# A graph network's attention edges, placed 17 tiles later: 27 chunks instead of 26

## The chip, the cores and the metric

The kernel runs on one core of one Trainium2 chip. TensorE (PE in the profile; its weight loads are PEld), VectorE (DVE), ScalarE (ACT), GpSimd (POOL) and SyncE (SP) are five engines with a queue each; they meet through semaphores. The metric is the time of one execution on the device, in microseconds; a kernel's time is the median over several executions.

## The reference

A graph has 6250 nodes with 128 features and 100000 edges, sorted by their destination. Destinations are drawn as 6250·u², so that low nodes have many edges and high ones few. Two relational layers come first (not touched by the change except that the lists for attention are made beside the first of them), and then two layers of graph attention, each followed by a batch normalization over the nodes and an ELU:

```python
src = jnp.concatenate([edge_index[0], loops])      # 100000 edges and 6250 self loops
dst = jnp.concatenate([edge_index[1], loops])
...
e = leaky_relu(al_s[src] + al_d[dst], 0.2)         # 4 heads
m = segment_max(e, dst)
ee = jnp.exp(e - m[dst])
den = segment_sum(ee, dst)
alpha = ee / den[dst]
out = segment_sum(alpha[:, :, None] * xw[src], dst)
...
mu, var = x.mean(0), x.var(0)                      # batch normalization, over all nodes
h = elu(gamma * (x - mu) * rsqrt(var + EPS) + beta)
```

## The kernel before

**Lists.** `gat_list` merges the sorted edges with the self loops into one list of 106250 entries, ordered by destination, and cuts it into tiles of 128. The constant `NT` = 832 is the number of tiles, `TC` = 32 the tiles of a chunk, `NCH` = 26 the chunks. 831 tiles hold entries; the last one is padding. `windows` finds for each group of `GQ` = 4 tiles the first node that it adds to, and counts how many passes over the list are needed (`passes_g`): one as long as the nodes of a group fit a window of `WA` = 68 columns; one more is added when the last chunk begins at a node below `SETTLED` = 5760, because the statistics of the batch normalization are taken of those nodes before the last chunk is summed. `chains` makes masks per chunk. All three are generators, stepped once in each half-group of the first relational layer (`rgcn`, `next(others, None)`), between that layer's own instructions. `rgcn` also fetches a row of relations per half-group into the tile `relT` (L733, four buffers) from SP's queue, three half-groups ahead.

**An attention layer** (`gat`, once for each of the two layers) has a fully unrolled loop over the chunks. Three things are written for a chunk k:

- `gathers(k)`: one indirect DMA a tile on POOL's queue (`gather`, L615), each bringing 128 rows of 136 numbers from the table in HBM into the tile `v`. `v` lies in two halves of 16 tiles; the pool `grp` has six buffers, so that three chunks have room. A half's buffer comes free when the chunk three before has been read from it.
- `softmax(k)`: a long chain of small instructions, mostly on DVE, with a few on PE and ACT between them. It begins with ACT's copies L853 and PE's transposes L855 of the whole chunk, so that the chunk's last gather must have landed; DVE's first instruction of it is L860; it ends with DVE L947 and the transposition L949 of the weights `w`.
- `sums(k)`: DVE weights eight tiles at a time (`weight`, L958) and makes one-hot selections (`selections`, L627); PE multiplies each tile with its selection (L974) into a bank for four tiles; DVE adds each bank to the sums (`add`, L961). It needs `softmax(k)`.

The order on the engines is that of the code (`in_order`): in loop k the gathers of chunk k+1 are written first (POOL runs as far ahead as the buffers allow), then 16 steps of `sums(k)`, two tiles a step; from the eighth step on, a piece of `softmax(k+1)` follows each step. The weights' transposition L949 of chunk k+1 is so the end of loop k. Only the next-to-last loop is different: there all of `sums` is written first, then the batch normalization's statistics (`bn_stats`, L1065) of the first 5760 nodes, 18 instructions, and then the last softmax by itself. After the last chunk follow two more instructions of statistics, `bn_factors` and the ELU.

Before the loops, `gat` copies one column per chunk into `snaps` (L1022, with register loads in between), takes the selections of the first tiles, and runs `gathers(0)` and `softmax(0)` with nothing beside them.

Of the kernel before, what the change touches and what calls it, by code (L numbers as in the profile page):

```python
# [8 lines left out]
F32 = mybir.dt.float32  # L9
# [28 lines left out]
ES = ER * SC  # L38
NT = 832
TC = 32  # L40
NCH = NT // TC
NP = NT // SC
G = 16
# [16 lines left out]
NS = 320  # L60
SETTLED = 18 * NS
FAR = 1e6
EPS = 1e-5
# [17 lines left out]
class Gnn:  # L81
# [214 lines left out]
    def gat_list(self, scratch):  # L296
# [3 lines left out]
        n = self.stage().bitcast(I32)  # L300
        nc.vector.tensor_scalar(n, self.self_d, float(N), None, op0=ALU.min)
        d = self.stage().bitcast(I32)
        nc.vector.tensor_scalar_add(d, n, float(KOFF))
        nc.vector.scalar_tensor_tensor(d, d, KDST, n, op0=ALU.logical_shift_left, op1=ALU.bitwise_or)
# [28 lines left out]
        nc.vector.tensor_scalar(cols(dst_i), turned, KDST, None, op0=ALU.logical_shift_right)  # L333
        self.dst = scratch[:, 5 * SW:5 * SW + NT]
        nc.vector.tensor_scalar(self.dst, dst_i, -float(KOFF), float(N), op0=ALU.add, op1=ALU.min)
# [6 lines left out]
    def windows(self, scratch):  # L342
# [9 lines left out]
        for q in range(NQ):  # L352
            first = dst[0:1, q * GQ * NP:(q * GQ + 1) * NP]
            nc.vector.tensor_copy(self.base[:, :, q], first)
            ps = self.ps()[:, :NP]
            nc.tensor.matmul(ps, self.ones, first, start=True, stop=True)
            w = slice(q * GQ * NP, (q + 1) * GQ * NP)
            of_group = lambda v: v.rearrange("e (c p) -> e c p", p=NP)
            nc.vector.tensor_sub(of_group(self.ahead[:, w]), of_group(dst[:, w]), ps[:, None, :].to_broadcast([P, GQ, NP]))
            starts.append((w, first))  # L360
# [12 lines left out]
        nc.vector.tensor_reduce(count[:, 1:2], steps, AX.X, ALU.add)  # L373
        c = column(NT - TC)
        nc.vector.tensor_scalar(count[:, 0:1], dst[0:1, c:c + 1], float(SETTLED), None, op0=ALU.is_lt)
        nc.vector.tensor_add(count[:, 1:2], count[:, 1:2], count[:, 0:1])
        self.passes_g = const.tile([1, 1], I32, name="passes")
        nc.vector.tensor_copy(self.passes_g, count[:, 1:2])
        yield
        nc.vector.tensor_copy(by_tile(firsts), by_place(dst[0:1, :]))  # L380
        nc.vector.memset(lasts[:, 0:1], -1.0)
        for w, first in starts:
# [16 lines left out]
    def chains(self, scratch):  # L399
# [35 lines left out]
        nc.vector.memset(self.cut[:, :, P:], 0.0)  # L435
        for k in range(0, NCH, 2):
            z = slice(k, k + 2)
            yield
            nc.vector.tensor_scalar(ri[:, z], ri[:, z], KDST, None, op0=ALU.logical_shift_right)
            nc.vector.tensor_scalar_mul(rows[:, z], ri[:, z], BIG)  # L440
            nc.vector.tensor_sub(self.cut[:, z, 1:P], rows[:, z, :P - 1], rows[:, z, 1:])
            for mask, e in ((self.head, 0), (self.tail, P - 1)):
                nc.vector.tensor_tensor(mask[:, z], rows[:, z], rows[:, z, e:e + 1].to_broadcast([P, 2, P]), ALU.is_equal)
        half = NCH // 2
        for k in range(0, NCH, half):
# [186 lines left out]
    def layer(self, body):  # L632

        nc, const = self.nc, self.const
        nc.vector.memset(self.moved, 0.0)
        passes = nc.values_load(self.passes_g, min_val=1, max_val=NZA + 1,
                                skip_runtime_bounds_check_because="a step of 0 is at most any width")
        self.in_order()
        with self.tc.For_i(0, passes):
            nc.vector.tensor_scalar(self.offset, self.ahead, self.moved, None, op0=ALU.subtract)  # L640

            groups = self.base.rearrange("o (k p) q -> o k (p q)", k=NCH)
            nc.vector.tensor_copy(self.start[:, :, 0:1], groups[:, :, 0:1])
            nc.vector.tensor_scalar(self.start[:, :, 1:], groups, self.moved[0:1, :], float(N), op0=ALU.add, op1=ALU.min)
            nc.vector.tensor_scalar_add(self.moved, self.moved, float(WA))
            body()
            self.in_order()
# [77 lines left out]
    def rgcn(self, acc, table, bs, wc, others=iter(()), post=None):  # L725
# [6 lines left out]
        def fetch(h):  # L732
            rel[h] = self.relp.tile([SC, P], F32, name="relT", bufs=4)  # L733
            nc.sync.dma_start(rel[h], self.rels[h * SW:(h + 1) * SW].rearrange("(g e) -> g e", e=P))
# [101 lines left out]
    def softmax(self, k):  # L836
# [113 lines left out]
        self.w, self.carry = w, sc[:, TC:]  # L950

    def sums(self, k, w, shrink):

# [5 lines left out]
        def add(i, ps):  # L959
            o = self.sum[:, bass.ds(at[i], WA)]  # L960
            nc.vector.tensor_add(o, o, ps[:, :WA])  # L961
        weight(0)
        at = self.registers(self.start[0:1, k, :])
# [3 lines left out]
        late = None  # L967
        for t in range(0, TC, 2):
            if t % GD == 0:
                s = self.s  # L970
            if t % GQ == 0:
                ps = self.ps()
            for i in range(t, t + 2):
                nc.tensor.matmul(ps[:, :WA], v[i // G][:, i % G, :D], s[:, i % GD, :],  # L974
                                 start=i % GQ == 0, stop=i % GQ == GQ - 1)
            if t % GD == 0:
                g = (k * TC + t) // GD + 1
                if g < NT // GD:
                    self.s = self.selections(g)
                if t + GD < TC:  # L980
                    weight(t + GD)
            if late:
                add(*late)
                late = None
            if t % GQ == GQ - 2:
                late = (t // GQ + 1, ps)
            if t == TC - 2:
                add(*late)
            yield
# [12 lines left out]
    def gat(self, table, others=iter(())):  # L1002
# [15 lines left out]
        self.snaps = self.chain.tile([P, NCH], F32, name="snaps")  # L1018
        for k in range(0, NCH, NCH // 2):
            at = self.registers(self.start[0:1, k:k + NCH // 2, 0])  # L1020
            for j in range(NCH // 2):
                nc.vector.tensor_copy(self.snaps[:, k + j:k + j + 1], self.sum[:, bass.ds(at[j], 1)])  # L1022

        def gathers(k):
            self.v[k] = [self.grp.tile([P, G, DG], F32, name="v", tag="grp") for z in range(2)]
            for i in range(TC):
                c = column(k * TC + i)
                if (k * TC + i) * P >= N + E:
                    nc.scalar.copy(self.v[k][i // G][:, i % G, :], self.zero.to_broadcast([P, DG]))
                    continue  # L1030
                self.gather(self.v[k][i // G][:, i % G, :], table, self.src_i[:, c:c + 1])

        self.s = self.selections(0)
        gathers(0)
        for _ in self.softmax(0):
            pass
        for k in range(NCH):
# [4 lines left out]
            soft = self.softmax(k + 1) if more else iter(())  # L1042
            if k == NCH - 2:

                for _ in adding:
                    next(others, None)
                self.bn_stats(0, SETTLED)

# [7 lines left out]
            for _ in soft:  # L1056
                pass
        for _ in others:
            pass
# [279 lines left out]
```

## Time and profile before

| | us |
|---|---|
| median of 9 runs | 5324.16 (5308.36 to 5336.65) |
| the profiled execution: its own time | 5337.72 |
| its span, first to last instruction | 5335.9 |
| first attention layer: first gather to last sum (L961) | 2469.3 to 3869.5 |
| second attention layer: first gather to last gather | 3903.7 to 5230.9 |
| busy over the span: PE, DVE, ACT, POOL | 2445.9, 2338.6, 453.1, 3067.3 |

The times inside the profile are counted from the span's start. Rows of the timeline give start, duration, engine, line, operation, tiles, shape and count; in square brackets stands the idle time of the engine before the row and what ended it by the semaphores' events. "remote" means that the wait ended on a semaphore event that the profile could not tie to an instruction; "issue" means that nothing seen in the profile was waited for. A matmul of f32 takes two passes, so that a tile is two L974 matmuls. The mean granted TensorE clock is 0.627 of full speed, 0.50 in the attention layers.

### The profile page before, as it was taken

How to read it: one execution, taken by the hardware profiler on the slowest of the kernel's cores; microseconds unless marked ns; L12 is line 12 of the kernel's file. 1: busy time of each engine (PE TensorE's matmuls, PEld its weight loads, DVE VectorE, ACT ScalarE, POOL GpSimd, SP SyncE). 2: the span in 40 equal slices, each digit the busy share in tenths (PEclk: the TensorE clock that was granted, in tenths of full speed). 3: DMA queues.
4: the chain of work that ended last, by engine and by line, in shares of the span. 5: the costliest groups of instructions: out<-in, count | busy, mean ns of one | idle time of the engine just before them, and what ended most of it. 6: DMA issues, size and time to landing. Idle time of an engine off the chain costs nothing.

```text
span 5335.9 us, 37837 instructions
## 1 busy us (share of the span) xinstructions
PE 2445.9 (46%) x9994; PEld 2058.9 (39%) x9994; DVE 2338.6 (44%) x6212; ACT 453.1 (8%) x715; POOL 3067.3 (57%) x3255
## 2 busy tenths in 40 slices
PE   2666666654666666663232323333422332333334
PEld 1555555553545555552232323323412232323324
DVE  4445565543445445553243433333533333433436
ACT  2110110110111111111000000000020000000002
POOL 4666666664666666663655556565255555656561
PEclk8777787776777777776555555555555555555555
DMA  3221121112221112122211111121121111112121
GB/s 104 55 54 48 47 62 49 50 50 65 56 54 50 48 52 54 52 58 63 48 41 44 42 42 44 42 45 40 22 67 43 43 43 42 45 40 46 42 46 33
DMA packets 154574, 262.89 MB, mean 49 GB/s; under 512 B 56557, under 2 KB 96330, under 8 KB 154348
## 3 DMA queue, kind: packets, MB, share of 16 engines
q0 software_dynamic: 103232, 218.43, 17.2%
q1 hardware_dynamic: 50884, 41.09, 2.5%
q8 instruction: 87, 1.43, 0.1%
q14 instruction: 139, 1.14, 0.1%
q10 hardware_dynamic: 232, 0.80, 0.1%
HBM read 239.52 MB, written 20.58 MB: 49 GB/s over the span
## 4 chain that ended last, share of the span: by engine, by line
another core or an unknown queue 32%; PE 27%; DVE 21%; issue 13%; POOL 3%; DVEq 1%; ACT 1%; DMA 0%; ACTq 0%; SPq 0%; POOLq 0%
PE ps L974 11%; PE ps L788 7%; PE ps L759 4%; DVE part L797 4%; POOL v L615 3%; DVE v L958 1%; PE ps L743 1%; PE ps L739 1%; DVE sw L751 1%; DVEq L620 1%; DVE hot L740 1%; DVE sel L746 1%; DVE own L894 1%; DVE acc L961 1%
## 5 line engine op out<-in xcount | busy, mean ns | idle before, releaser
L615 POOL DMA_INDIRECT v<-gtable,src_i x1662 | 1571.8, 946 | 1187.5 <-issue 1101.0
L615 POOL DMA_INDIRECT v<-htable,src_e x1564 | 1488.3, 952 | 902.7 <-issue 439.0
L974 PE MATMUL ps<-selg,v 128*128 128x68 f32 x3328 | 787.2, 423 | 91.9 <-DVE v L958 86.0
L788 PE MATMUL ps<-sw,v 128*128 128x192 f32 x3128 | 739.6, 400 | 150.4 <-issue 50.7
L974 PEld LDWEIGHTS ps<-selg,v 128*128 128x128 f32 x3328 | 742.7, 331 | 138.4 <-DVE v L958 95.9
L788 PEld LDWEIGHTS ps<-sw,v 128*128 128x128 f32 x3128 | 660.1, 238 | 195.0 <-issue 70.6
L797 DVE TENSOR_TENSOR part<-part,ps 128x192 f32 x1564 | 553.0, 354 | 319.9 <-remote 125.0
L961 DVE TENSOR_TENSOR acc<-acc,ps 128x68 f32 x416 | 92.7, 223 | 977.0 <-remote 730.5
L759 PE MATMUL ps<-part,basis 128*128 128x288 f32 x1568 | 483.3, 470 | 2.4 <-DVE part L797 2.4
L938 PE MATMUL ps<-part,of_head 4*128 4x65 f32 x104 | 34.1, 428 | 886.3 <-DVE acc L961 759.4
L743 PE MATMUL ps<-wc,hot 128*128 128x64 f32 x392 | 107.8, 368 | 718.1 <-DVE hot L740 527.1
L759 PEld LDWEIGHTS ps<-part,basis 128*128 128x128 f32 x1568 | 344.4, 226 | 104.3 <-issue 2.8
L743 PEld LDWEIGHTS ps<-wc,hot 128*128 128x128 f32 x392 | 82.3, 255 | 771.8 <-DVE hot L740 560.0
L938 PEld LDWEIGHTS ps<-part,of_head 4*128 4x128 f32 x104 | 25.7, 305 | 896.2 <-issue 805.3
L751 DVE TENSOR_TENSOR sw<-sel,ps 128x1536 f32<-128x1536 f32 x196 | 343.8, 1754 | 26.1 <-remote 11.0
L754 ACT COPY part<-zero 128x2304 f32<-128x2304 f32 x98 | 206.9, 2111 | 1648.6 <-remote 938.2
L764 DVE TENSOR_TENSOR acc<-acc,ps 128x288 f32 x98 | 44.6, 455 | 660.9 <-remote 482.6
L465 PE MATMUL ps<-sel,head_of 128*4 128x32 f32 x208 | 44.6, 312 | 603.2 <-DVE sel L463 300.3
L958 DVE TENSOR_TENSOR v<-v,w 128x1024 f32<-128x1024 f32 x208 | 252.3, 1213 | 11.5 <-issue 3.5
L465 PEld LDWEIGHTS ps<-sel,head_of 128*4 128x4 f32 x208 | 9.4, 84 | 623.8 <-DVE sel L463 307.2
L627 DVE TENSOR_TENSOR selg<-nodes,offset 128x544 f32<-128x544 f32 x208 | 149.2, 717 | 0.1
L885 ACT ACTIVATE e<-e 128x128 f32<-128x128 f32 x52 | 16.1, 309 | 1469.9 <-issue 718.5
(307 smaller groups left out, 1898.8 us busy)
## 6 DMA issues: line engine op xcount, KB each, us to landing
v<-gtable,src_i POOLq DMA_INDIRECT x1662
v<-htable,src_e POOLq DMA_INDIRECT x1564
htable<-x SPq DMA_DIRECT2D x7, 448.0 KB
relT<-rels SPq DMA_DIRECT2D x196, 4.0 KB
acc<-xtable SPq DMA_DIRECT2D x7, 448.0 KB
x<-in_x_dram SPq DMA_DIRECT2D x7, 441.0 KB
acc<-htable SPq DMA_DIRECT2D x12, 256.0 KB
gtable<-flags SPq DMA_DIRECT2D x11, 272.0 KB
```

What stands on the lines that cost most here:

```text
L615: self.nc.gpsimd.indirect_dma_start(out=out, out_offset=None, in_=table, in_offset=bass.IndirectOffsetOnAxis(ap=idx, axis=0))
L627: self.nc.vector.tensor_tensor(s, self.nodes[:, None, :].to_broadcast([P, GD, WA]), self.offset[:, g:g + (GD - 1) * NP + 1:NP, None].to_br ...
L743: nc.tensor.matmul(coef[h][:, P:P + SC * NBASE], t, wc.rearrange("p g b -> p (g b)"), start=True, stop=True)
L751: nc.vector.tensor_tensor(x, s[:, :, None, :].to_broadcast(shape), c[:, :, :, None].to_broadcast(shape), ALU.mult)
L754: nc.scalar.copy(x, self.zero[:, :, None].to_broadcast([P, NBASE, WG]))
L759: nc.tensor.matmul(ps[:, :WG], bs[:, b, :], x[:, b, :], start=b == 0, stop=b == NBASE - 1)
L788: nc.tensor.matmul(ps[:, (j - i) * NBASE * W:(j - i + 1) * NBASE * W], v[:, j, :], sw[h][:, j].rearrange("p b w -> p (b w)"), start=True, ...
L797: nc.vector.tensor_add(o, o, x.rearrange("p (b w) -> p b w", b=NBASE))
L938: nc.tensor.matmul(ps[:, :2 * TC + 1], self.of_head, part, start=True, stop=True)
L958: nc.vector.tensor_mul(x, x, wz[:, :, :, None].to_broadcast([P, GD, H, FH]))
L961: nc.vector.tensor_add(o, o, ps[:, :WA])
L974: nc.tensor.matmul(ps[:, :WA], v[i // G][:, i % G, :D], s[:, i % GD, :], start=i % GQ == 0, stop=i % GQ == GQ - 1)
```

## The change

Seventeen tiles of padding are put ahead of the list (entries with the node -1, clipped to 0 where an address is made of it), so `NT` is 864 and `NCH` 27. The first chunk holds 15 tiles with entries (17 to 31), the last holds 16 (832 to 847); the 831 tiles between are cut at other places than before. Tiles without entries are not gathered but filled with zeros by ACT in one or two copies a chunk, and `sums` leaves them out. All of `sums` is interleaved with the next softmax in every loop, also in the next-to-last one. The statistics are taken in three parts: 15 instructions after loop 23 (nodes below 4800, which adds a second condition to the number of passes), 3 after loop 25, and the last 2 at the end. The masks in `chains` are made in 9 steps of 3 chunks instead of 13 of 2 and in 3 parts instead of 2; `snaps` is loaded in 3 parts instead of 2; `relT` has three buffers instead of four.

```diff
+SHIFT = 17
+LIVE = -(-(N + E) // P)
-NT = 832
+NT = 864
+EARLIER = 15 * NS
...
 # gat_list
-        nc.vector.tensor_scalar(n, self.self_d, float(N), None, op0=ALU.min)
+        nc.vector.tensor_scalar(n, self.self_d, float(N + SHIFT * P), float(SHIFT * P), op0=ALU.min, op1=ALU.subtract)
         d = self.stage().bitcast(I32)
-        nc.vector.tensor_scalar_add(d, n, float(KOFF))
+        nc.vector.tensor_scalar(d, n, -1.0, float(KOFF), op0=ALU.max, op1=ALU.add)
+        nc.vector.tensor_scalar(n, n, 0.0, None, op0=ALU.max)
...
 # windows
-            first = dst[0:1, q * GQ * NP:(q * GQ + 1) * NP]
+            first = scratch[0:1, (4 + q) * NP + 3 * NT:(5 + q) * NP + 3 * NT]
+            nc.vector.tensor_scalar(first, dst[0:1, q * GQ * NP:(q * GQ + 1) * NP], 0.0, None, op0=ALU.max)
...
+        for chunks, node in ((1, SETTLED), (3, EARLIER)):
+            c = column(NT - chunks * TC)
+            nc.vector.tensor_scalar(count[:, 0:1], dst[0:1, c:c + 1], float(node), None, op0=ALU.is_lt)
+            nc.vector.tensor_add(count[:, 1:2], count[:, 1:2], count[:, 0:1])
...
 # rgcn
-            rel[h] = self.relp.tile([SC, P], F32, name="relT", bufs=4)
+            rel[h] = self.relp.tile([SC, P], F32, name="relT", bufs=3)
...
+    def live(self, k):
+        return max(SHIFT - k * TC, 0), min(SHIFT + LIVE - k * TC, TC)
 # sums
+        lo, hi = self.live(k)
+        begin = lo // GD * GD
+        weight(begin)
-        for t in range(0, TC, 2):
+        for t in range(begin, hi, 2):
...
-            for i in range(t, t + 2):
+            for i in range(max(t, lo), min(t + 2, hi)):
...
 # gat
-        for k in range(0, NCH, NCH // 2):
+        for k in range(0, NCH, NCH // 3):
...
-            for i in range(TC):
+            lo, hi = self.live(k)
+            for z, v in enumerate(self.v[k]):
+                a, b = (min(max(x - z * G, 0), G) for x in (lo, hi))
+                for w in (slice(0, a), slice(b, G)):
+                    if w.start < w.stop:
+                        nc.scalar.copy(v[:, w, :], self.zero[:, :, None].to_broadcast([P, w.stop - w.start, DG]))
+            for i in range(lo, hi):
...
-            if k == NCH - 2:
-                for _ in adding:
-                    next(others, None)
-                self.bn_stats(0, SETTLED)
...
+            if k == NCH - 4:
+                self.bn_stats(0, EARLIER)
+            if k == NCH - 2:
+                self.bn_stats(EARLIER, SETTLED)
```

## The prediction

> **What bounds the kernel now.** I read the page first. Its chain that ended last gives a third of the span to no engine:
>
> ```profile
> another core or an unknown queue 32%; PE 27%; DVE 21%; issue 13%; POOL 3%; DVEq 1%; ACT 1%; DMA 0%; ACTq 0%; SPq 0%; POOLq 0%
> L615 POOL DMA_INDIRECT v<-gtable,src_i x1662 | 1571.8, 946 | 1187.5 <-issue 1101.0
> ```
>
> The timeline around the start of the first attention layer says where that third comes from. First the rows of all engines, then PE's, then DVE's.
>
> ```profile
> 2469.27 0.94 POOL L615 DMA_INDIRECT v<-gtable,src_i  x1 [70.49 <-DVE start L644]
> 2470.52 0.95 POOL L615 DMA_INDIRECT v<-gtable,src_i  x1 [0.30 <-issue]
> ...
> 2512.09 0.29 DVE L860 SCALAR_TENSOR_TENSOR own<-cut,ps 128x128 f32<-128x128 bf16 x1 [28.22 <-issue]
> ...
> 2525.39 0.21 DVE L912 TENSOR_TENSOR ex<-ps,big 4x64 f32<-4x64 f32 x1 [2.62 <-remote]
> ```
> ```profile
> 2553.41 0.47 PE L949 MATMUL w<-ident,e 128*128 128x128 f32 x1 [8.41 <-DVE e L947]
> 2560.44 3.69 PE L974 MATMUL ps<-selg,v 128*128 128x68 f32 x16 [1.56 <-issue]
> 2625.21 0.47 PE L949 MATMUL w<-ident,e 128*128 128x128 f32 x1 [6.00 <-DVE e L947]
> ```
> ```profile
> 2575.82 0.23 DVE L961 TENSOR_TENSOR acc<-acc,ps 128x68 f32 x1 [15.05 <-remote]
> 2596.12 0.23 DVE L961 TENSOR_TENSOR acc<-acc,ps 128x68 f32 x1 [20.07 <-remote]
> 2604.05 0.28 DVE L860 SCALAR_TENSOR_TENSOR own<-cut,ps 128x128 f32<-128x128 bf16 x1
> ```
>
> Gathers are issued every 1.25 us. PE had finished the first 16 tiles' matmuls by 2564.1, yet DVE learned of the 8th tile at 2575.8 and of the 12th at 2596.1: four tiles in 20 us, so 5 us for each of PE's signals. While gathers run, the other engines' signals come late. POOL issued 96 gathers in one run up to 2589.2, and only 14.7 us after that the rest came at once. Steady loops show the same smaller, and the end shows the engines without gathers:
>
> ```profile
> 3757.53 1.98 PE L974 MATMUL ps<-selg,v 128*128 128x68 f32 x8
> 3766.88 0.94 POOL L615 DMA_INDIRECT v<-gtable,src_i  x1 [0.30 <-issue]
> 3771.62 0.23 DVE L961 TENSOR_TENSOR acc<-acc,ps 128x68 f32 x1 [12.83 <-remote]
> 3779.37 0.47 PE L949 MATMUL w<-ident,e 128*128 128x128 f32 x1 [0.74 <-DVE e L947]
> 3781.34 0.94 POOL L615 DMA_INDIRECT v<-gtable,src_i  x1 [13.52 <-issue]
> ...
> 3818.05 13.92 PE L974 MATMUL ps<-selg,v 128*128 128x68 f32 x64 [1.69 <-DVE v L958]
> 3832.26 7.18 DVE L1065 BATCH_NORM_STATS2 bn_st<-acc 128x6 f32<-128x320 f32 x18
> 3839.36 0.27 DVE L860 SCALAR_TENSOR_TENSOR own<-cut,ps 128x128 f32<-128x128 bf16 x1
> ```
>
> A loop lasts (3779.4 − 2625.2) / 22 = 52.5 us: 32 gathers are 40 us, then some 12.5 us in which the chain finishes at full speed while POOL waits for the buffer that this loop frees. So neither data nor an engine's busy time bounds the layer. It is the chain of softmax and sums, slowed by gathers beside it. Without gathers a softmax from L860 to L949 takes 14.2 us (3839.4 to 3853.5); with gathers throughout, 41.3 (2512.1 to 2553.4).
>
> **The steps.** I compare the moments at which L949 ends a loop. From here "the first full loop" is the first whose sums have 32 tiles: loop 0 before, loop 1 after.
>
> *The head.* Seventeen gathers fewer precede the first softmax: 17 × 1.25 = 21.2 us, so its L949 comes at 2553.4 − 21.2 = 2532.2 if the softmax is slowed as before. ACT's zero fill (2304 columns take 2.1 us in L754's row) lies beside 19 us of gathers. The three-part load of `snaps` lies there too; it ended at 2483.2, against an L860 now due at 2490.9: 8 us of cover, up to 4 us lost if a third load adds a 3 us wait.
>
> *The added loop 0.* It holds the sums of 15 tiles and then the softmax of chunk 1, with nothing to overlap them. POOL does not pause meanwhile: chunks 0 to 2 and the first half of chunk 3, whose buffer held only zeros, are 15 + 32 + 32 + 16 = 95 gathers in one run, up to 2588. Late signals clear with the run's length: 14.7 us after 96, 3.5 to 4.9 after 32, 2.7 after 16 (2624.6 to L961 at 2627.3). So L860 comes at about 2602.7; PE's own pace gives the same, 13 signals at 5 us after the first five, 2533 + 65. From L860 to L949 the same stretch took 21.2 us (2604.05 to 2625.2) with 16 gathers beside it; a little less here, with no sums between: 20. Loop 0 ends at 2623. Bounds: 14.2 instead of 20 and earlier signals give 2600; a run that never pauses because its signals come in time reaches 111 gathers, ends at 2608, clears 17 us later, and gives 2629.
>
> *Loop 1.* The gathers of chunk 4's first half wait for these sums' first half, so only 16 lie in this loop. L949 to L860: 2.9 to the first matmul, 7.1 for 32 of them, 0.6 for L855: 10.6. Then 21.2 as above. It ends at 2623 + 31.8 = 2654.8; before, the first full loop's start was already reached at 2625.2. So the list's middle starts 29.6 us later, and the 22 steady loops that follow are the same in both, with the same gathers in each.
>
> *The tail.* Before, from L949 at 3779.4: 35.8 us with 15 gathers, then 15.6 of sums alone, 7.2 of statistics, 14.2 of softmax, 2 and 13.9 of sums, ending at 3869.2: 89.8 us. After, POOL is done when loop 24 starts. A free interleaved loop is 10.6 + 4.5 to L472 + 12.4 (L472 at 3802.7 to 3815.1) = 27.5. The statistics only change places: 15 × 0.40 = 6.0 stand on DVE before loop 24's first weighting, where PE has nothing else, and 3 × 0.40 = 1.2 before the last sums; what was 7.2 is 7.2. The last sums are 16 tiles: 2.9 + 7.0. Together 6.0 + 27.5 + 27.5 + 1.2 + 9.9 = 72.1, a gain of 17.7. ACT's fill of the last half chunk stands behind the softmax's copies in its queue and has 10 us before L853; its cost is taken as nothing (2 us a layer if late).
>
> *A layer* costs 29.6 − 17.7 = +11.9 us, and both, the second having the same rows (4058.9 − 3903.7 = 155.2 from first gather to that L949, against 155.9), +23.8.
>
> *The lists.* One DVE instruction of 0.7 us is added in the merge, two clips (0.2 each), three counts (0.13 each), and 1/27 more masks (13 steps of 1.8 us before, so +0.9): 2.4 us. DVE is 51% busy in that stage, and the work is spread over half-groups; I take 2 of 2.4, at least 0. Three steps fewer shift ACT's clearing earlier, at no cost. `relT`'s fetch now waits for the matmul L739 three half-groups before its use instead of four. Behind it on SP are table stores and loads of later data. The least time between such matmuls after the start is 25 us in the rows, against some 15 us for a late signal and 3 for the load: nothing, with up to 5 us if the cover is gone.
>
> *The sum*: 5337.7 + 23.8 + 2 = 5363.5 for a profiled execution; the median stands 0.25% under it, so 5350.
>
> A page of the Trainium skill speaks for the other sign. "TensorE: Matmul & The Clock Gate", section "The cost: per-tile semaphore tail", prices one increment of a semaphore at 26.3 ns, serialized. By that, 16 increments end in half a microsecond, loop 0 would cost a free loop of some 25 us, and the estimate from the page would be about the faster rival below. The rows show 20 us for four, so the rows decide.
>
> **The rivals.** *Faster: the added loop escapes the slowing.* The first softmax slowed down at 2521, 51 us after its run of gathers began, but only 9 us after its own start; steady loops slow 10 to 12 us after POOL resumes, with many more instructions beside it. If what counts is how much has piled up, the shorter head lets this softmax through: L949 at 2490.9 + 14.2 = 2505. The sums are then done at once, chunk 1 lands at 2530, its softmax ends at 2547, and the next loop lasts as long as the old first one, 71.8: 2619, or −6 against before. With the tail −24 a layer: 5337.7 − 48 + 2, so 5278 as a median. For it speaks that the free rows are so short; against it, that POOL keeps issuing without a pause to 2608, where signals have always been late. It decides where loop 1 ends before about 2637 (2625.2 + 17.7, less 6.3 a layer for the bound below).
>
> *Slower by more: loop 1 is steady at once.* If POOL's run reaches 111 gathers and chunk 4 joins without a pause, loop 0 ends at 2629 and loop 1 lasts 52.5: 2681.5, +56.3 − 17.7 = +38.6 a layer, 5403.
>
> *No change that shows:* loops 0 and 1 each some 6 us shorter than I have them, by a weaker slowing, so +11.9 − 12 a layer: 5326, the same within 0.2% (some 11 us, about what a measurement can tell from no change).
>
> *A second pass*, where a group exceeds 68 nodes or chunk 24 begins below node 4800. By the draw, entries below node n number 100000·√(n/6250) + n; chunk 24 begins at entry 96128, node 5163. At nine entries a node at the end, four tiles span 57. Improbable; it would cost over 2600 us.
>
> **How the numbers follow.** Forecast 0.46, centre 5350, its own range 5334 to 5370; faster rival 0.25; no change 0.12; slower by more 0.16; second pass 0.01. The bound to faster is 5313.5, to slower 5334.8. Faster takes the first rival and a little of its neighbour, 0.27; same takes its case and the forecast's lower edge, 0.15; slower the rest, 0.58. The range reaches from just under the faster rival, 5274, to the slower one, 5403.
>
> **What would show it.** Right: L860 of the second softmax not before some 2595, although the first gathers end at 2487; a run of 95 or more gathers from 2469; loop 1 near 32 us; no POOL row after loop 23; L949 to L949 of 27 us in loops 24 and 25; L1065 in runs of 15, 3 and 2 with idle PE beside the 15. Wrong: a first L949 near 2505 and a second near 2547, steady loops of another length than 52.5, late loops of over 35 us, a change in the relational stages beyond 5 us, or each L615 form executed twice.

## The result, and the profile after

The changed kernel took 5337.88 us (median of 16 runs, 5330.32 to 5348.17) against 5324.59 us for the kernel before on the same chip: a ratio of 1.0026, 95% interval [1.0018, 1.0034], 13.3 us slower. The profiled execution's span went from 5335.9 to 5357.5 us; it is one execution of each kernel, and the one after took 5359.24 us, 21 us above its median (before: 13 us above), so the rows below show 8 us more of a difference than the medians do. Two further measurements on other chips (among the experiments below) gave 1.0013 [1.0001, 1.0025] and 1.0016 [1.0005, 1.0027].

The changed kernel's lines have moved: the gather is L622, the softmax's first DVE step L867, the transposition that ends a loop L956, the sums' matmul L987, the add L972, the weighting L969, the statistics L1081. "w" below is the moment at which L956 starts. A run of gathers is taken to end 0.3 us after its last row, the gap that follows every gather.

The chain that ended last, of the page after, has hardly another composition than before:

```profile
another core or an unknown queue 32%; PE 26%; DVE 22%; issue 14%; DVEq 1%; ACT 1%; POOL 1%; DMA 0%; ACTq 0%; SPq 0%; POOLq 0%
```

The head of the first layer, from the timeline: PE's rows of w, DVE's rows of loop 0, POOL's first row and its rows at the end of its first run.

```profile
2530.64 0.48 PE L956 MATMUL w<-ident,e 128*128 128x128 f32 x1 [7.72 <-issue]
...
2628.77 0.47 PE L956 MATMUL w<-ident,e 128*128 128x128 f32 x1 [1.80 <-DVE e L954]
...
2660.42 0.47 PE L956 MATMUL w<-ident,e 128*128 128x128 f32 x1 [5.95 <-DVE e L954]
```
```profile
2547.48 0.23 DVE L972 TENSOR_TENSOR acc<-acc,ps 128x68 f32 x1 [9.91 <-remote]
...
2568.48 0.23 DVE L972 TENSOR_TENSOR acc<-acc,ps 128x68 f32 x1 [20.77 <-remote]
...
2590.88 0.23 DVE L972 TENSOR_TENSOR acc<-acc,ps 128x68 f32 x1 [22.17 <-remote]
...
2596.48 0.29 DVE L867 SCALAR_TENSOR_TENSOR own<-cut,ps 128x128 f32<-128x128 bf16 x1 [5.37 <-remote]
```
```profile
2469.57 0.94 POOL L622 DMA_INDIRECT v<-gtable,src_i  x1 [70.15 <-DVE start L651]
...
2586.95 0.94 POOL L622 DMA_INDIRECT v<-gtable,src_i  x1 [0.30 <-issue]
2591.58 0.94 POOL L622 DMA_INDIRECT v<-gtable,src_i  x1 [3.69 <-issue]
```

Loop 0 lasts 98.1 us for the sums of 15 tiles and one softmax. PE had finished its matmuls by 2542, and DVE learns of four tiles at a time only 21 to 22 us apart, until POOL's run of 95 gathers ends at 2588.2. POOL then stops for no more than 3.7 us. Loop 1 lasts 31.6 us, and full loops of 52.5 us begin.

The tail of the first layer: PE's w and the sums that follow the statistics, then the POOL rows at the pause in it, then DVE's statistics.

```profile
3763.82 0.47 PE L956 MATMUL w<-ident,e 128*128 128x128 f32 x1 [0.75 <-DVE e L954]
...
3797.28 0.47 PE L956 MATMUL w<-ident,e 128*128 128x128 f32 x1 [0.75 <-DVE e L954]
...
3805.98 7.09 PE L987 MATMUL ps<-selg,v 128*128 128x68 f32 x32 [7.47 <-DVE v L969]
...
3839.44 0.47 PE L956 MATMUL w<-ident,e 128*128 128x128 f32 x1 [0.75 <-DVE e L954]
...
3865.35 0.48 PE L956 MATMUL w<-ident,e 128*128 128x128 f32 x1 [0.75 <-DVE e L954]
```
```profile
3784.52 0.94 POOL L622 DMA_INDIRECT v<-gtable,src_i  x1 [0.30 <-issue]
3799.25 0.94 POOL L622 DMA_INDIRECT v<-gtable,src_i  x1 [13.79 <-issue]
```
```profile
3798.80 6.00 DVE L1081 BATCH_NORM_STATS2 bn_st<-acc 128x6 f32<-128x320 f32 x15
```

Loop 23 lasts 33.5 us and not 52.5: POOL issues 16 gathers in it, to 3785.8, and the last 16 only in loop 24, from 3799.25 on. Loop 24 lasts 42.2 us with the statistics (PE idle 7.47 us ahead of its first sums) and these gathers, loop 25 without either 25.9. The last sum ends at 3876.7.

A layer, from its first gather, against the kernel before:

| us, in the profiled executions | first softmax and loops 0, 1 (before: loop 0) | the next 22 loops | the rest | sum |
|---|---|---|---|---|
| predicted | +29.6 | 0 | −17.7 | +11.9 |
| layer 1 | 190.8 − 155.9 = +34.9 | 1136.9 − 1154.2 = −17.3 | 79.4 − 90.1 = −10.7 | +6.9 |
| layer 2 | 187.9 − 155.2 = +32.7 | 1146.1 − 1152.5 = −6.4 | 79.4 − 90.2 = −10.8 | +15.5 |

### The profile page after: what moved, and what is told of

Same layout as the page of the kernel before. It is cut to its first block, busy times and chain, and to the rows that moved or that the text cites. A ratio compares the mean times of both kernels' runs of the same rounds, so it can differ in the third digit from the quotient of the medians.

```text
span 5357.5 us, 37986 instructions
## 1 busy us (share of the span) xinstructions
PE 2460.8 (46%) x10014; PEld 2071.1 (39%) x10014; DVE 2363.4 (44%) x6292; ACT 463.6 (9%) x733; POOL 3065.9 (57%) x3255
## 4 chain that ended last, share of the span: by engine, by line
another core or an unknown queue 32%; PE 26%; DVE 22%; issue 14%; DVEq 1%; ACT 1%; POOL 1%; DMA 0%; ACTq 0%; SPq 0%; POOLq 0%
PE ps L987 10%; PE ps L795 6%; PE ps L766 4%; DVE part L804 4%; DVE v L969 1%; PE ps L750 1%; DVE sw L758 1%; POOL v L622 1%; PE ps L746 1%; DVEq L627 1%; DVE hot L747 1%; DVE own L901 1%; DVE sel L753 1%; DVE acc L972 1%
## 5 line engine op out<-in xcount | busy, mean ns | idle before, releaser
L622 POOL DMA_INDIRECT v<-gtable,src_i x1662 | 1572.7, 946 | 1233.6 <-issue 1107.4
L622 POOL DMA_INDIRECT v<-htable,src_e x1564 | 1486.0, 950 | 905.8 <-issue 440.4
L987 PE MATMUL ps<-selg,v 128*128 128x68 f32 x3324 | 788.8, 423 | 110.6 <-DVE v L969 103.3
L795 PE MATMUL ps<-sw,v 128*128 128x192 f32 x3128 | 750.9, 404 | 168.0 <-issue 67.5
L987 PEld LDWEIGHTS ps<-selg,v 128*128 128x128 f32 x3324 | 743.3, 331 | 157.8 <-DVE v L969 113.6
L972 DVE TENSOR_TENSOR acc<-acc,ps 128x68 f32 x416 | 92.5, 222 | 999.9 <-remote 751.0
L969 DVE TENSOR_TENSOR v<-v,w 128x1024 f32<-128x1024 f32 x208 | 252.2, 1213 | 12.2 <-issue 4.7
```

The lines of the kernel that those rows point to most:

```text
L622: self.nc.gpsimd.indirect_dma_start(out=out, out_offset=None, in_=table, in_offset=bass.IndirectOffsetOnAxis(ap=idx, axis=0))
L795: nc.tensor.matmul(ps[:, (j - i) * NBASE * W:(j - i + 1) * NBASE * W], v[:, j, :], sw[h][:, j].rearrange("p b w -> p (b w)"), start=True, ...
L969: nc.vector.tensor_mul(x, x, wz[:, :, :, None].to_broadcast([P, GD, H, FH]))
```

## The experiments

The theory under test is that the head's loss, and the length of every full loop, come from other engines' signals being late while POOL issues gathers one behind the other. The first rival is that the added loop costs what it does by its own work, sums and softmax one after the other. Edits are given in short form. The experiments ran on several chips. On one of them (e5 to e8) the kernel before took 4295 us, on the others 5247 to 5335 us; each ratio is to the kernel before on the same chip, and the text says where that matters.

**The zero fill behind the gathers (e1).** It asks why loop 23 was short.

```
         for each half: a, b = its live tiles
-            ACT zero fill of what isn't live        # ahead of the gathers (for k = 0 it stays there)
         for i in range(lo, hi): gather tile i
+        if k > 0: the same zero fill                # behind them
```

> The changed kernel with one thing moved: the last chunk's zero fill stands after its gathers in the program instead of ahead of them, so that the gathers take the buffer that is free after the first half of loop 23's sums. Theory (the number of gathers beside a loop sets its length, and more than in proportion: 25.9 us with none, 33.5 with 16, 52.5 with 32): the last 16 gathers follow the 16 before them at once, loop 23 lasts 52.5 instead of 33.5, loop 24 with its 6 us of statistics 33 instead of 42.2, loop 25 stays at 26: +10 us a layer, some 20 us in all, 5358. Rival (a loop pays for its gathers in proportion, some 0.8 us each): 33.5 + 42.2 only changes to 52.5 + 33 less some 10, the same sum: 5338. Second rival (the tail's gain comes from the statistics' new places alone): loops 23 to 25 keep their sum, 5338.

Measured: 1.0059 [1.0043, 1.0076], against 1.0013 to 1.0026 for the change: some 17 to 24 us more. PE's w at the tail, here and in the next experiment, which has the change's own tail and ran on the same chip:

```profile
3694.20 0.47 PE L956 MATMUL w<-ident,e 128*128 128x128 f32 x1 [0.75 <-DVE e L954]
...
3746.55 0.47 PE L956 MATMUL w<-ident,e 128*128 128x128 f32 x1 [0.75 <-DVE e L954]
...
3778.23 0.47 PE L956 MATMUL w<-ident,e 128*128 128x128 f32 x1 [0.75 <-DVE e L954]
...
3804.14 0.47 PE L956 MATMUL w<-ident,e 128*128 128x128 f32 x1 [0.74 <-DVE e L954]
```
```profile
3694.18 0.48 PE L956 MATMUL w<-ident,e 128*128 128x128 f32 x1 [0.75 <-DVE e L954]
...
3729.60 0.47 PE L956 MATMUL w<-ident,e 128*128 128x128 f32 x1 [0.75 <-DVE e L954]
...
3771.41 0.47 PE L956 MATMUL w<-ident,e 128*128 128x128 f32 x1 [0.74 <-DVE e L954]
...
3797.32 0.48 PE L956 MATMUL w<-ident,e 128*128 128x128 f32 x1 [0.75 <-DVE e L954]
```

Loops 23 to 25 last 52.4, 31.7 and 25.9 us, together 110.0. In the next experiment they last 35.4, 41.8 and 25.9, together 103.1. So 32 gathers in one loop and none in the next cost 7 us more than 16 and 16, against 10 expected; the rivals gave nothing. That is 14 us in two layers; the rest of the 17 to 24 is not seen in the rows, and the profiled execution, at 5246.06 us, was one of the shortest of eight (5233.67 to 5282.63). The order of two instructions decides it. With the fill behind, POOL issues 32 gathers in one run in loop 23 (3696.2 to 3736.2); with the fill ahead, the last 16 start 13.8 us after the others, at the start of loop 24. This fits buffers that are handed out in the order of first use: a fill ahead takes the buffer that is free in the middle of loop 23 and leaves the gathers the one that is free at its end.

**Chunk 3's gathers held in loop 0 (e2).** It shortens POOL's first run from 95 to 79 gathers and moves nothing else.

```
+        if k == 3: gpsimd.tensor_copy(held, ends[0:1, 0, 2*TC:2*TC+1])   # written by the second softmax's L874
         for i in range(lo, hi): gather tile i
```

> The changed kernel, with the 16 gathers of chunk 3's first half held back on POOL until the second softmax has written its first scan over tiles (L874 in the changed kernel's numbering of this run). Nothing else is moved. Theory (loop 0 is slow because POOL issues 95 gathers without a pause): the run is 79 gathers and ends at 2569 instead of 2588; late signals clear 12 us after it, so L867 of the second softmax comes near 2580 instead of 2596.5, and w of loop 0 near 2600 to 2605 instead of 2628.8. Chunk 3's gathers then lie beside loop 1, which may lengthen from 31.6 to at most 52.5 us: w of loop 1 between 2633 and 2655 instead of 2660.4, a gain of 5 to 27 us a layer, 5284 to 5328. Rival (loop 0 costs what it does because sums and softmax stand one after another, whatever POOL does): w of loop 0 stays at 2628, 5338.

Measured: 0.9979 [0.9968, 0.9990]. POOL's row with the wait, DVE's L867, PE's first three w, and the same three w of the experiment above, where nothing is held:

```profile
2561.37 0.20 POOL L1047 COPY held<-ends 1x1 f32<-1x1 f32 x1 [13.94 <-DVE ends L874]
```
```profile
2559.71 0.28 DVE L867 SCALAR_TENSOR_TENSOR own<-cut,ps 128x128 f32<-128x128 bf16 x1
```
```profile
2509.19 0.48 PE L956 MATMUL w<-ident,e 128*128 128x128 f32 x1 [7.73 <-DVE e L954]
...
2574.01 0.48 PE L956 MATMUL w<-ident,e 128*128 128x128 f32 x1 [1.91 <-DVE e L954]
...
2630.37 0.48 PE L956 MATMUL w<-ident,e 128*128 128x128 f32 x1 [5.22 <-DVE e L954]
```
```profile
2507.20 0.48 PE L956 MATMUL w<-ident,e 128*128 128x128 f32 x1 [7.73 <-DVE e L954]
...
2605.36 0.47 PE L956 MATMUL w<-ident,e 128*128 128x128 f32 x1 [1.80 <-DVE e L954]
...
2631.90 0.48 PE L956 MATMUL w<-ident,e 128*128 128x128 f32 x1 [2.51 <-DVE e L954]
```

The run of 79 ended at 2547.7, and L867 came 12.0 us later, as expected (79 × 0.153 = 12.1). From it to w it took 14.3 us, as without gathers. Loop 0 fell from 98.2 us (the experiment above, same chip) to 64.8; the rival needed it unchanged. Loop 1, which now has the held gathers beside it, rose from 26.5 to 56.4, so that by its end 3.5 us of the 33.4 were left (4.0 in layer 2), under the 5 expected at the least. The time fell by 0.3 to 0.5% against the change; how much of that is these 2 × 4 us and how much the difference between chips stays open.

**The new tail on the old layout (e3).**

```
-            if k == NCH - 2: drain the sums, then bn_stats(0, SETTLED)
+            behind each loop: if k == NCH - 4: bn_stats(0, EARLIER)
+                              if k == NCH - 2: bn_stats(EARLIER, SETTLED)
```

> The kernel before with the tail part of the change alone: no tiles are moved, the next-to-last loop is interleaved like the others, and the statistics of the first 15 groups of nodes stand after loop 22, of 3 more after loop 24, of the last 2 at the end. Theory (the tail's parts add up loop by loop): loop 23 with 15 gathers takes 35.8 and 4 to 6 for the statistics, loop 24 has no gathers and takes 26, then 1.2 of statistics and 15.9 of sums, 83 to 85 against 89.8 us in the kernel before: 5 to 7 us a layer, 5311 to 5315. So of the 30.6 us of layer 1's tail in the changed kernel no more than a quarter is the statistics' and the interleaving's, the rest the shorter last chunk and the gathers spread over two loops. Rival (the interleaving is the larger part, as 15.6 + 14.2 us of work one after another become 26): 10 us or more a layer, under 5305.

Measured: 0.9987 [0.9974, 1.0000], some 5 to 7 us, where 10 to 14 were expected; the interval holds both these and nothing. In its profile loop 23 lasts 40.5 us, loop 24 25.9 and the rest to the last sum 18.1: 84.5 against 90.1 before, 5.6 us a layer, as the theory had it. The rival's 10 us a layer are excluded. So most of the tail's 28 us in layer 1 come from the shorter last chunk and from the gathers' place.

**A pause after every fourth gather, in the changed kernel (e4).** It leaves the number of gathers and the order of all work as they are, and spaces the gathers from 1.25 to 1.417 us.

```
         gather tile i
+        if i % 4 == 3: gpsimd.iota(pause, pattern=[[0, 800]])
```

> The changed kernel, with a pause on POOL after every fourth gather of both attention layers: an index fill of 1x800 elements, some 0.8 us by the rows of the fills at hand (1x261 0.35 us, 128x1024 0.98). So 32 gathers take 46.4 us instead of 40. Theory (other engines' signals are late because POOL issues gathers a little faster than something behind it works them off: late signals clear 0.15 us after a run for each gather in it, which makes 1.40 us a gather against 1.25 issued): at 1.45 us a gather nothing piles up, the first softmax takes 14 to 16 us, loop 0 some 30, a full loop is set by POOL alone, 46.5 to 48.5 us instead of 52.5, and a layer takes 831 x 1.45 = 1205 us and some 30 after its last gather: 1235 to 1270 instead of 1407. 5338 - 2 x (137 to 172) = 4994 to 5064. Rival (each gather delays the others by itself, however far apart they are): the pauses only add to POOL's 40 us, loops stay at 52.5 or go to 59: 5338 to 5620.

Measured: 0.9424 [0.9402, 0.9445], 4939.27 us: by far the largest effect of all, with more work on POOL, not less. First POOL's rows, then PE's w in the head, then DVE's group of the adds with its idle time, for the changed kernel and for this one:

```profile
2903.40 0.94 POOL L622 DMA_INDIRECT v<-gtable,src_i  x1 [0.30 <-issue]
2904.35 0.78 POOL L1050 IOTA pause<- 1x800 int32 x1
2905.30 0.94 POOL L622 DMA_INDIRECT v<-gtable,src_i  x1 [0.16 <-issue]
```
```profile
2479.40 0.47 PE L956 MATMUL w<-ident,e 128*128 128x128 f32 x1 [1.82 <-DVE e L954]
...
2524.67 0.47 PE L956 MATMUL w<-ident,e 128*128 128x128 f32 x1 [1.82 <-DVE e L954]
```
```profile
L972 DVE TENSOR_TENSOR acc<-acc,ps 128x68 f32 x416 | 92.5, 222 | 999.9 <-remote 751.0 <-PE ps L987 196.1 <-issue 51.3
```
```profile
L972 DVE TENSOR_TENSOR acc<-acc,ps 128x68 f32 x416 | 92.0, 221 | 180.5 <-PE ps L987 174.8 <-remote 5.3 <-issue 0.5
```

The adds sat idle 999.9 us, 751 of them up to remote signals, and now 180.5 and 5.3. Loop 0 takes 45.3 us instead of 98, full loops 45.4, which is POOL's 32 × 1.417 and nothing besides, and POOL never stops: 831 gathers in 1177.3 us, the last sum 33.3 us behind them. The rival, that each gather delays the others however far apart they are, would have lengthened the loops.

**The same pause in the kernel before (e5)** (the same two lines).

> The kernel before (tiles not moved) with the same pause of 1x800 after every fourth gather of the attention layers. Theory (the changed head costs its 35 us a layer only because the signals are late there): with signals on time both kernels are set by POOL, 831 x 1.417 = 1177.7 us from a layer's first gather to the end of its last, and differ only in what follows it. In the changed kernel with pauses that was 33 us (3619.4 to 3652.4). Here the last softmax can't start before the last gather has landed either, 5 us after it, then 14.2 us of softmax, 2 and 13.9 us of sums and 0.5: 35 to 36 us. So it ends 2 to 4 us a layer later than the changed kernel with pauses: 0.9424 to 0.945 of the kernel before, and the change, which cost 0.26%, now gains some 0.1%. Rival (an extra loop in the head costs by its own work): the kernel before with pauses is faster than the changed one with pauses by what the change cost, 13 to 70 us: 0.930 to 0.940.

This ran on the chip where the kernel before takes 4294.89 us, so its ratio, 1.0631 [1.0617, 1.0646], answers another question than it was meant to: the pause is a pure loss there. The one meant can be read from the profiles, as POOL sets the pace at 1.417 us in both. The first gather and the last add of the first layer, here and in the changed kernel with pauses:

```profile
2071.39 0.94 POOL L615 DMA_INDIRECT v<-gtable,src_i  x1 [28.32 <-DVE start L644]
3282.38 0.23 DVE L961 TENSOR_TENSOR acc<-acc,ps 128x68 f32 x1 [1.48 <-PE ps L974]
```
```profile
2441.74 0.94 POOL L622 DMA_INDIRECT v<-gtable,src_i  x1 [70.75 <-DVE start L651]
3652.13 0.23 DVE L972 TENSOR_TENSOR acc<-acc,ps 128x68 f32 x1 [1.48 <-PE ps L987]
```

A layer takes 1211.2 and 1210.9 us here, and 1210.6 and 1208.5 in the changed kernel with pauses. So the changed one is ahead by 0.6 and 2.4 us, where the theory said 2 to 4; the rival needed the kernel before to be ahead by 6 us a layer or more. The two ran on different chips, and 831 gathers at one pace set the length of both: the pair shows that the added loop costs nothing behind them, not what its work takes by itself.

**Half the pause (e6, e11), and the pause in the head alone (e7, e10)**, in the changed kernel: the fill is 1x400 after every fourth gather, or 1x800 in chunks 0 to 3 (`and k <= 3`). Both ran on that chip and then on others.

> The changed kernel with half the pause: a fill of 1x400, some 0.45 us by the rows of the fills, after every fourth gather, so about 1.33 us a gather. Theory (something behind POOL works off one gather in 1.40 us): at 1.33 us gathers still pile up, 0.07 us each; the signals come late by a little that grows until POOL has to wait for a buffer, and a full loop settles where the work behind POOL sets it, 32 x 1.40 = 44.8 us, or a little above: 45 to 47 us. About what the full pause gives, 0.940 to 0.950 of the kernel before. Rival (what counts is that POOL stops at all after a few gathers, so that the others' signals pass in each pause): a loop takes 32 x 1.33 = 42.6 to 43 us, 0.92 to 0.925.

> The changed kernel with the full pause (1x800 after every fourth gather) in chunks 0 to 3 alone; the rest issues as before. Theory (the changed head is slow by the run of 95 gathers): first gather to first w 38 us as in the kernel with pauses throughout, loop 0 45 us instead of 98, loop 1 45 to 53 instead of 31.6, then loops of full length again (50 to 53 us); the end of loop 1 comes 128 to 136 us after the first gather instead of 190.8, and the tail is unchanged: 55 to 63 us a layer, 0.979 to 0.984 of the kernel before where the changed kernel has 1.0026. Rival (what is saved in the head is given back where POOL, now later, has not run ahead): the loops after it lengthen until the same point, under 20 us a layer: over 0.994.

Measured on the chip with 4294.89 us: 1.0284 [1.0270, 1.0298] and 1.0086 [1.0073, 1.0100]. Neither theory nor rival was tested by it, as there is nothing late there. PE's w of two neighbouring loops without pauses, and the group of the adds, of the second kernel:

```profile
2610.75 0.48 PE L956 MATMUL w<-ident,e 128*128 128x128 f32 x1 [0.81 <-DVE e L954]
...
2650.92 0.48 PE L956 MATMUL w<-ident,e 128*128 128x128 f32 x1 [0.81 <-DVE e L954]
```
```profile
L972 DVE TENSOR_TENSOR acc<-acc,ps 128x68 f32 x416 | 92.2, 222 | 132.6 <-PE ps L987 132.4 <-issue 0.3
```

A loop is 40.1 us, 32 × 1.25, with the same gathers at the same distance as in the slow loops; no wait of the adds ends on a remote signal. With half the pause it is 42.5, 32 × 1.33.

> The changed kernel with the half pause (1x400 after every fourth gather, 1.33 us a gather) again. Where the kernel before takes over 5200 us, theory (something behind POOL works off one gather in about 1.40 us, and what POOL issues faster piles up): POOL issues at 1.33 us but is held back later for buffers, loops settle at 45 to 47 us with signals late in part, 0.940 to 0.955 of the kernel before. Rival (each short stop lets the others' signals pass): loops of 42.5 us, as where signals are on time, 0.915 to 0.925. Where the kernel before is near 4300 us: 1.0284 as before, loops of 42.5.

Where the kernel before takes 5323.39 us: 0.9572 [0.9555, 0.9588], a little beyond the theory's 0.940 to 0.955 and far from the rival. Full loops (2 to 22) average 47.7 and 46.9 us in the two layers, and loop 0 lasts 106 us, longer than without any pause, though loop 1 ends sooner, 178.7 and 178.4 us after the first gather (191.5 and 188.8 in the changed kernel on this chip): at 1.33 us signals are still late, at 1.417 they no longer are.

> The changed kernel with the pauses in chunks 0 to 3 alone, again. Where the kernel before is near 5250 to 5320 us and its loops take over 50 us, theory (the changed head is slow by the run of 95 gathers): loop 0 45 us instead of 98, loop 1 45 to 53 instead of 31.6, then loops of full length, 55 to 63 us less a layer, 0.979 to 0.984. Rival (what the head saves is given back by loops that POOL has not run ahead of): over 0.994. Where the kernel before is near 4300 us: 111 pauses of 0.17 us a gather add 18.5 us a layer, 1.0086 as before.

Where the kernel before takes 5334.59 us: 0.9962 [0.9948, 0.9975], on the rival's side, 29 us under the change on that chip. The head did what the theory said: loops 0 and 1 last 45.4 and 47.0 us, and loop 1 ends 130.2 us after the first gather (189.1 in the changed kernel on this chip). PE's next w show what the rival said:

```profile
2605.90 0.48 PE L956 MATMUL w<-ident,e 128*128 128x128 f32 x1 [1.12 <-DVE own L953]
...
2680.93 0.48 PE L956 MATMUL w<-ident,e 128*128 128x128 f32 x1 [20.25 <-issue]
```

POOL, which had nothing to wait for, issued 48 gathers without a pause behind the spaced ones, and loops 2 and 3 took 75.0 and 65.7 us in layer 1. By the end of loop 3 only 25 us of the 59 were left in layer 1, 16 in layer 2.

**Pauses in the whole kernel (e8)**, the relational layers included (three fills of 1x8 after every fourth gather):

> The changed kernel with three very short fills (1x8) after every fourth gather of the whole kernel, the relational layers' gathers too; by the rows some 0.3 us together, about 1.33 us a gather. In the relational layers 16 gathers take 20 us and a round 22.8 us, and DVE waits 13 us of it for remote signals. Theory (late signals there too): a round comes down to 16 x 1.40 = 22.4 at most a little less, so 0 to 0.4 us for each of 98 rounds, and the attention layers do as with the half pause: 0.935 to 0.950. Rival (in the relational layers the short runs of 16 let a pause clear the signals at once): a round of 16 x 1.33 = 21.3, some 150 us less: 0.89 to 0.92.

1.0778 [1.0763, 1.0792], on the chip where nothing is late, so that what was expected was not tested; whether the relational layers gain where signals are late was not seen. There the three short fills cost more than the half pause: 1.35 to 1.38 us a gather in the attention layers.

**The change again (e9, e12)**, on two further chips:

> The changed kernel as it is, once more beside the kernel before, since the runs before this one fell on chips on which the kernel before took 5247 and 4295 us. Theory (the change's cost is all late signals): where the kernel before is near 4300 us and its full loops take 40.1 us, 32 x 1.25, the engines are on time, both kernels are set by POOL's 831 gathers a layer, and what differs is the end of a layer, 1 to 2 us shorter in the changed kernel, and its lists, some 2 us longer: 0.9985 to 1.0010. Where the kernel before is near 5250 to 5320 us: 1.001 to 1.004, as at first. Rival (the added loop costs by its own work, wherever it runs): 1.0026 or more in both.

> The changed kernel once more, for the condition that the two runs so far didn't meet. Where the kernel before is near 4300 us, theory (the change's cost is late signals alone): loops 0 to 24 of 40 us in both kernels, a layer from its first gather to its last sum some 1 to 2 us shorter in the changed kernel, lists 2 us longer: 0.9985 to 1.0010. Rival (the added loop costs by its own work): 1.0026 or more. Where the kernel before is over 5200 us: 1.001 to 1.003.

1.0013 [1.0001, 1.0025] beside 5334.59 us, and 1.0016 [1.0005, 1.0027] beside 5323.39 us, both within what was expected for chips with late signals. Loops 0 and 1 lasted 98.3 and 30.3, 96.7 and 32.4 us, loops 23 and 24 34.2 and 42.1, 34.8 and 42.0. The change itself did not come onto the chip with signals on time; that it makes no difference there rests on the paced pair above.

## Why the prediction was right where it was, and where it was not

The sign and the mechanism of the head held: beside a run of 95 gathers the added loop took 98 us, with a run of 79 (e2) 65, with spaced gathers (e4) 45. The median came 12 us below the 5350 forecast, near the lower end of the forecast's own range (5334 to 5370), and the kernel lost half of what was forecast, 13 us instead of 26. The profiled execution fitted better, 5359.24 us against 5363.5; but the median stands 0.40% under it, and not 0.25%. That the sum fits so well is in part luck: the head cost 3 to 5 us a layer more than forecast, middle and tail together gained 10 us more in layer 1 and nothing more in layer 2, and the errors nearly cancel (22.4 us for both layers, forecast 23.8).

*The head* was forecast at +29.6 us and cost 34.9 and 32.7. The first w came at 2530.6 (2532.2 forecast), POOL's run was 95 gathers to 2588.2 (95 to 2588), loop 1 31.6 us (31.8). Between them two terms missed in opposite directions. L867 came at 2596.5, 8 us after the run and not 14.7. Then L867 to L956 took 32.3 us and not 20, since POOL resumed after 3.7 us, before the signals had cleared. The row that I took for that stretch had 15 us of silence ahead of it.

*The middle and the tail*: the step "POOL is done when loop 24 starts" was wrong. I had assumed that the last chunk's gathers follow the buffers as the others' do, and did not see that its fill, ahead of them, takes the earlier buffer. So loop 23 lasted 33.5 us instead of 52.5 and loop 24 42.2 instead of 33.5; e1 shows that this is the cause and that it was worth some 7 us a layer. The sign "no POOL row after loop 23" and that of 27 us for loop 24 failed with it, and one of the signs of being wrong, a late loop of over 35 us, came true. In layer 2 loop 23 lasted 37.1 us, and the other full loops averaged 52.8 us against 52.4 before, which took back 9 us; whether that is the change or this one execution is not shown. The other tail terms held: 6.0 and 1.28 us for the statistics, 25.9 us for a free loop (27.5), 11.3 us from the last w to the last sum (11.1). ACT's fill of the last half (2.01 us at 3837.73) delayed nothing that is seen.

*The lists* were put at +2 us; the first gather came at 2469.6 instead of 2469.3, in one execution each; that DVE's added steps lie beside other waits there was not tested.

*The rivals.* The faster one needed the first w near 2505. It came at 2530.6: DVE's steps slowed some 9 us after this softmax's own start again, at the same step of the chain, though POOL's run was only 31 us old by then (51 before). That rival supposed that the length of the run decides; these rows speak against it. The rival "slower by more" needed a run of 111 gathers; it was 95.

The prediction weighed a sentence of the Trainium skill ("TensorE: Matmul & The Clock Gate", section "The cost: per-tile semaphore tail", 26.3 ns for an increment, serialized) against 20 us for four tiles. The experiment with pauses (e4) puts the two together: with signals on time the last adds of loop 0 come 1.7 us apart, PE's own pace for eight matmuls (6.67 us for 30), and a price as small as the page's could not be seen there. So no run here shows the 26.3 ns; what the runs show is that, with gathers at 1.25 us on a chip with late signals, four tiles took 20 us, and the page's price alone does not give the time.

## What to carry to other kernels

Where "remote" ends an engine's waits while another engine issues indirect DMAs at a steady pace, space the issues a little before rearranging anything: here 0.17 us a gather brought 5.8% on a chip with late signals, and moving tiles lost 0.1 to 0.3%. But measure it on more than one chip: the same pause, in the kernel before, cost 6.3% where signals were on time. And count a step that fills a buffer as a user of that buffer: its place in the program decides which transfer starts early.

## What the hardware showed that was not expected

*Late signals go with the chip, not with the kernel.* The same kernel before took 4295 us on one chip and 5247 to 5335 on the others, at granted clocks of 0.62 to 0.64 in all profiles. POOL's gather takes 0.94 us and comes every 1.25 us on both kinds; on the fast one no wait of the adds ends on a remote signal (e7), and a full loop is 40.1 us instead of 50 to 53. The view of DMA issues there gives 2.5 us from a gather's issue to its landing; on the others it gives no such time. The chip with signals on time was seen in one sitting (e5 to e8), so whether this is the chip or its state at that time stays open, and what differs these runs do not say.

*The gathered data is not late.* The traces also hold the DMA's packets. The last of a gather's 32 packets ends 2.2 us after its issue (median of the first layer: 2.23 us in the kernels before and after, 2.15 to 2.16 in the other runs, on both kinds of chip), and for the 95th gather of the changed kernel's run it is 2.23 us as well. So what falls behind is not the transfer, only the signals. With it goes a gap in the record: the traces hold 55 614 to 55 620 semaphore events of DMAs on the chip with signals on time, and 11 056 to 12 625 on the others (24 993 with the full pause). So "remote" there may tell of a missing record as much as of the sender, and what shows the lateness is the lengths of the loops; whether missing records and late signals have one cause was not tested.

*Between two paces signals begin to fall behind.* At 1.25 and 1.33 us a gather they are late on such a chip, at 1.417 they are not. The time in which they clear grows with the run before it (14.7 us after 96 gathers, 12.0 after 79, 2.7 after 16). As an estimate from these, 0.15 to 0.17 us a gather on top of 1.25, something works a gather off in about 1.40 us; what that is was not found. A backlog that grows with every gather does not explain all rows: in the first softmax the late steps came at the same distances (1.2 and 2.9 us of idle time) whether POOL's run was 31 us old or 51. More gathers beside a loop cost more than in proportion: 25.9 us with none, 33.5 with 16, 52.5 with 32.
